# A decoder on one core: the results of sorted expert tiles in a buffer of their own, and the shared experts last in the order

## The chip, the core and the metric

One core of a Trainium2 chip runs the whole program in one launch. The metric is the device time in microseconds. The kernel before was run three times: 835.97, 840.87 and 841.37, median 840.87. The profile is of one more execution, which took 843.06 us and whose span, from its first to its last instruction, is 841.28 us.

## What is computed

Two decoder layers on x of 16 sequences, 128 positions and 256 channels, in fp32. Layer 0: causal attention with one head, attention to a context with 16 heads, and an FFN of 16 blocks of which a router picks four. Layer 1: self attention and windowed attention with 16 heads, and the part that matters here, a mixture of eight experts:

```python
shared_out = _swiglu(x, ws_gate, ws_up, ws_down)           # for every token
scores = jax.nn.sigmoid(x @ gate_weight.T)
topk_w, topk_idx = jax.lax.top_k(scores, 2)                # two of eight experts
topk_w = topk_w / (topk_w.sum(-1, keepdims=True) + 1e-20) * 2.5
g = jnp.einsum('th,eih->tei', x, w_gate)
u = jnp.einsum('th,eih->tei', x, w_up)
y = jnp.einsum('tei,ehi->teh', jax.nn.silu(g) * u, w_down)
out = jnp.einsum('te,teh->th', combine, y) + shared_out    # combine holds topk_w
```

and `x = x + out`.

## The kernel before

The 16 sequences are cut into eight *lanes* of two sequences. A lane is a chain of stages, each a Python generator; up to five lanes are under way at once. The order of instructions on every engine is fixed when the program is built: `Turns` keeps, for each engine, the time up to which it has been given work, and, for each kind of buffer, when its slots come free (`LIMITS`, line 383: six of `p`, four of `xe`, four PSUM banks `bank`, three of `tmp`). Each `yield ENGINE, dict(tag=n)` asks for an engine and for n slots; `q.give(tag)` gives one back. `Turns.run` takes the request that can start first, and at equal times the one of lower *rank*; that is the number that `q.start(generator, rank, at)` sets. Its estimates of cost only set the order: on the chip each engine goes through its own list in that order and waits on semaphores.

The last FFN is done in two ways.

*Dense* (`expert_ffn`, lanes 5, 6 and 7; tensors x5 to x7): all eight experts and the two shared ones, ten rounds of `gu` (four matmuls of 128x256, two for the gate and two for the up projection), `sg` (tanh on ACT), two DVE operations to `hm`, and for the eight experts `wb`, a matmul that spreads the token's weight, with one more DVE operation. Ten matmuls `y` per sequence and a sum on DVE end it, then a store of the lane to the output.

*Sorted* (lanes 0 to 4): `routing` sends each token's row to its two experts' places in DRAM (`to_experts`, indirect DMAs on POOL). When all five lanes are routed, `plan` works out 27 tiles of 128 rows with one expert each, and `sorted_experts` runs `expert_tile` 27 times: two gathers by indirect DMA on POOL (768 columns of the expert's weights, 256 of the rows), transposes `xgt`, a copy `xgT` on ACT, matmuls `gu2`, `sg2` on ACT, two DVE operations to `h2`, a transpose `hT2`, a copy, the matmul `y2`, a copy to the result `yo` on ACT, and a store to `by_experts` in DRAM, issued by ACT. Weights, rows and result share one buffer of kind `p`, 1024 columns wide: the result overwrites the rows, behind the weights. Kind `p` also holds the exponentials of the attentions. `xe` holds `xgT`.

`shared` does the two shared experts of a sorted lane (`gu`, `y1` with `L_shared`); it is started by `layer_1` when the lane is routed. When all five shared parts and all 27 tiles are done (`part_ended`), `combining` starts for the five lanes: a few small DVE operations for the places, four gathers from `by_experts` per lane on POOL (20 in all), a DVE sum for each, and a store of the lane to the output on SP.

In the profile a tile goes by its name without number: `we<-in_L_experts` and `we<-to_experts` are the two gathers, `by_experts<-we` the store, `yg` combining's gathers, `gu<-we,xgT` the matmuls gu2, `y<-we,hT` y2, `ptt` the transpose of a dense lane's (or layer 0's) router weights, `kb` the spread keys of an attention. Most instructions have the line of a helper (135 matmul, 140 transpose, 144 DVE, 149 ACT, 155 POOL, 168 indirect DMA, 189 a load or store).

Of the kernel before, what the change touches and what calls it, by code (L numbers as in the profile page):

```python
# [17 lines left out]
B, S, D = 16, 128, 256  # L18
P = 128
DC = D // P  # L20
G = 2
NL = B // G
# [52 lines left out]
PE, DVE, ACT, POOL, SP = "PE", "DVE", "ACT", "POOL", "SP"  # L75
# [197 lines left out]
def decoder(ctx: ExitStack, tc: tile.TileContext, a: dict, out: bass.AP):  # L273
# [10 lines left out]
    def bank(shape, name):  # L284
        return ps.tile(shape, F32, tag="bank", name=name)
# [101 lines left out]
    q = Turns(nc, LIMITS)  # L387

    def new(tag, shape, name, dtype=F32):
        return work.tile(shape, dtype, tag=tag, name=name, bufs=LIMITS[tag])  # L390

    def normalise(src, free=False):

        yield DVE
        mv = small.tile([P, G, 2], F32, tag="mv", name="mv")
        for j in range(G):
            st = small.tile([P, 6], F32, tag="st", name="st")
            q.dve("bn_stats", st, src[:, j, :])
            q.dve("bn_aggr", mv[:, j, :], st)
        yield POOL  # L400
        rstd = small.tile([P, G], F32, tag="rstd", name="rstd")
        q.pool("tensor_scalar", rstd, mv[:, :, 1], EPS, None, ALU.add)
        q.pool("tensor_tensor", rstd, rstd, power, ALU.pow)

        less = small.tile([P, G], F32, tag="less", name="less")
        q.pool("tensor_tensor", less, mv[:, :, 0], rstd, ALU.mult)
        q.pool("tensor_scalar", less, less, -1.0, None, ALU.mult)
        yield DVE, dict(xn=1)
        xn = new("xn", [P, G, D], "xn")

        def one(j):
            if j:
                yield ACT
                q.act("activation", xn[:, j, :], src[:, j, :], AF.Identity, bias=less[:, j : j + 1], scale=rstd[:, j : j + 1])
            else:
                yield DVE
                q.dve("tensor_scalar", xn[:, j, :], src[:, j, :], mv[:, j, 0:1], rstd[:, j : j + 1], ALU.subtract, ALU.mult)

        yield [one(j) for j in range(G)]
        if free:  # L420
            q.give("xn")
        return xn
# [12 lines left out]
    def transposed(src, free=True):  # L435
        t = yield from transposed_psum(src, free)
        yield ACT, dict(xT=1)
        sb = new("xT", [P, DC, GT], "srcT")
        q.act("copy", sb, t)
        q.give("bank")  # L440
        return sb
# [427 lines left out]
    def self_attention(l):  # L869

        xn = yield from normalise(x[l])
        xT = yield from transposed(xn, free=False)

        def residual():
            for j in range(G):

                yield POOL
                q.pool("tensor_tensor", xn[:, j, :], xn[:, j, :], row("L1_attn_b_o"), ALU.add)
                q.pool("tensor_tensor", x[l][:, j, :], x[l][:, j, :], xn[:, j, :], ALU.add)
            q.give("xn")  # L880

        def of_keys():
            kT = yield from keys(w["qkv"], D, xT, "L1_attn_b_k")
            return (yield from spread(kT))

        kb, qT, v, _ = yield [
            of_keys(),
            queries(w["qkv"], 0, xT, "L1_attn_b_q", 0.0625),
            values(w["qkv"], 2 * D, xT, "L1_attn_b_v"),
            residual(),  # L890
        ]
        q.give("xT")

        def one(j):
            on = yield from attention(qT, kb, v, j)
            yield from output_projection(on, w["o1"], l, j, free="on")

        yield [one(j) for j in range(G)]
        q.give("qk")
        q.give("kb")  # L900
        q.give("v")
        v_tiles.append(v)
# [108 lines left out]
    def shared(l):  # L1011

        g = group_of[l]

        xT = yield from transposed((yield from normalise(x[l])))
        yield PE, dict(hm=1)
        hm = new("hm", [P, DC, GT], "hm1")

        def one(f):
            yield PE, dict(bank=1, tmp=1)  # L1020
            gu = bank([P, 2, GT], "gu")
            for n in range(2):
                at = n * D + f * P
                for d in range(DC):
                    q.matmul(gu[:, n, :], w["shared"][:, d, at : at + P], xT[:, d, :], start=d == 0, stop=d == DC - 1)
            yield from gated(gu, hm[:, f, :])

        yield [one(f) for f in range(DC)]
        q.give("xT")
        for j in range(G):  # L1030
            yield PE, dict(bank=1)
            y = bank([P, D], "y1")
            for f in range(DC):
                q.matmul(y, hm[:, f, j * S : (j + 1) * S], w["shared"][:, f, 2 * D :], start=f == 0, stop=f == DC - 1)
            if j == G - 1:
                q.give("hm")
            yield DVE
            q.dve("tensor_tensor", x[l][:, j, :], x[l][:, j, :], y, ALU.add)
            q.give("bank")
        part_ended(g)  # L1040

    def part_ended(g):

        g.parts -= 1
        if g.parts == 0:
            at = q.now.at
            for l in g.lanes:
                q.start(combining(g, l), 2 * NL + l, at)
# [44 lines left out]
    def expert_tile(g, i):  # L1093

        yield POOL, dict(p=1)

        we = new("p", [P, HC, S], "we").rearrange("p h s -> p (h s)")
        xg = yo = we[:, 3 * D :]
        q.indexed(we[:, 0 : 3 * D], None, a["L1_experts"], g.tile_weights[:, i : i + 1])
        yield POOL  # L1100
        q.indexed(xg, None, g.to_experts, g.tile_rows[:, i : i + 1])
        yield PE, dict(bank=1)
        t = bank([P, DC, S], "xgt")
        for d in range(DC):
            q.transpose(t[:, d, :], xg[:, d * P : (d + 1) * P], ident)
        yield ACT, dict(xe=1)
        xgT = new("xe", [P, DC, S], "xgT")
        q.act("copy", xgT, t)
        q.give("bank")
        yield PE, dict(bank=1, tmp=1)  # L1110
        gu = bank([P, 2, P], "gu2")
        for d in range(DC):
            wt = we[:, d * D : (d + 1) * D].rearrange("p (n f) -> p n f", f=P)
            q.matmul(gu, xgT[:, d, :], wt, start=d == 0, stop=d == DC - 1)
        q.give("xe")
        yield ACT
        sg = new("tmp", [P, P], "sg2")
        q.act("activation", sg, gu[:, 0, :], AF.Tanh, scale=0.5)
        yield DVE, dict(p0=1)
        h = new("p0", [P, P], "h2")  # L1120
        q.dve("scalar_tensor_tensor", sg, sg, 1.0, gu[:, 0, :], ALU.add, ALU.mult)
        q.dve("scalar_tensor_tensor", h, sg, 0.5, gu[:, 1, :], ALU.mult, ALU.mult)
        q.give("tmp")
        q.give("bank")
        yield PE, dict(bank=1)
        t = bank([P, P], "hT2")
        q.transpose(t, h, ident)
        q.give("p0")
        yield ACT, dict(pT0=1)
        hT = new("pT0", [P, P], "hT")  # L1130
        q.act("copy", hT, t)
        q.give("bank")
        yield PE, dict(bank=1)
        y = bank([P, D], "y2")
        q.matmul(y, hT, we[:, DC * D : 3 * D], start=True, stop=True)
        q.give("pT0")
        yield ACT
        q.act("copy", yo, y)
        q.give("bank")
        q.load(g.by_experts[i * P : (i + 1) * P, :], yo, engine=ACT)  # L1140
        q.give("p")

    def combining(g, l):

# [40 lines left out]
    def gated(gu, h):  # L1185

        yield ACT
        sg = new("tmp", [P, GT], "sg")
        q.act("activation", sg, gu[:, 0, :], AF.Tanh, scale=0.5)
        yield DVE  # L1190
        q.dve("scalar_tensor_tensor", sg, sg, 1.0, gu[:, 0, :], ALU.add, ALU.mult)
        q.dve("scalar_tensor_tensor", h, sg, 0.5, gu[:, 1, :], ALU.mult, ALU.mult)
        q.give("tmp")
        q.give("bank")
# [122 lines left out]
    def sorted_experts(g):  # L1317
        yield from plan(g)
        yield [expert_tile(g, i) for i in range(g.tiles)]
        part_ended(g)  # L1320
# [86 lines left out]
    def layer_1(l):  # L1407
        yield from self_attention(l)
        yield from windowed_attention(l)
        ended.append((1, l))  # L1410
        g = group_of.get(l)
        if g is not None:
            yield from routing(l)
            g.left -= 1
            at = q.now.at
            q.start(shared(l), 2 * NL + l, at)
            if g.left == 0:
                q.start(sorted_experts(g), 2 * NL + min(g.lanes), at)

# [127 lines left out]
```

## Time and profile before

| What | us |
|---|---|
| runs, median of three | 840.87 (835.97 to 841.37) |
| profiled execution | 843.06, span 841.28 |
| TensorE (PE) busy | 782.0 (93%) |
| DVE, ACT, POOL busy | 479.2, 393.0, 450.4 |
| first and last gather of an expert tile issued | 649.0, 778.5 |
| last store of a tile issued | 800.55 |
| combining's first and last gather issued | 804.76, 828.67 |
| last matmul, last output store issued | 833.5, 837.9 |

The times in the traces are counted from the span's start. In the page, "busy" is an engine's time in instructions; "PE" is matmuls and "PEld" the loads of their weights, which run beside them. A matmul in fp32 has two records. In the timeline a line is: start, duration, engine, line, operation, out<-in, count, and in brackets how long the engine had been idle before it and what ended that. In the list of waits a line is: who waited, for what, total us, how often, longest. The granted clock of PE was 0.979 in the mean.

### The profile page before, as it was taken

To read this page: it belongs to the slowest core of one execution; us is meant where nothing else is said; L and a number is where in the kernel's file an instruction comes from. 1 tells how busy PE (TensorE), PEld (TensorE's weight loads), DVE (VectorE), ACT (ScalarE), POOL (GpSimd) and SP (SyncE) were. 2 spreads that over 40 slices of the span, in tenths; PEclk is the share of its full clock that TensorE was granted. 3 is DMA by queue.
4 is the path that set the end of the run, shared out by engine and by line. 5 is a ranking of instruction groups with operands and counts; after the bars stand their busy time and mean duration, and the time that the engine had idled before them with its cause. 6 is when DMAs were issued, how large, how long until landed. Compare 5 with 4: busy or idle time off the path is not lost.

```text
span 841.3 us, 19812 instructions
## 1 busy us (share of the span) xinstructions
PE 782.0 (93%) x7886; PEld 617.5 (73%) x7886; DVE 479.2 (57%) x1257; ACT 393.0 (47%) x874; POOL 450.4 (54%) x720
## 2 busy tenths in 40 slices
PE   6999999999999999999999999999878699989984
PEld 5777678878778677777777777777656477877862
DVE  4455636546626537656785478578485553364263
ACT  4545355344355364646652755646545234333310
POOL 5325535514335266566776756966764843474053
PEclk9999899999999999999999999999999999999997
DMA  8457440601201011010013111101201533455133
GB/s 287 157 149 221 133 134 29 182 17 35 57 3 38 14 58 33 15 51 14 20 46 128 63 44 52 59 26 51 77 21 32 163 101 111 129 163 164 57 93 119
DMA packets 60940, 70.41 MB, mean 84 GB/s; under 512 B 8848, under 2 KB 52496, under 8 KB 60208
## 3 DMA queue, kind: packets, MB, share of 16 engines
q1 hardware_dynamic: 51584, 46.20, 17.7%
q0 software_dynamic: 5376, 19.40, 7.9%
q10 hardware_dynamic: 3888, 3.54, 1.2%
q8 instruction: 62, 1.02, 0.5%
q14 instruction: 30, 0.25, 0.1%
HBM read 43.96 MB, written 20.97 MB: 77 GB/s over the span
## 4 chain that ended last, share of the span: by engine, by line
PE 76%; DVE 9%; POOL 5%; ACT 4%; issue 3%; another core or an unknown queue 2%; DMA 0%; ACTq 0%; POOLq 0%; DVEq 0%
PE s L135 15%; PE y L135 11%; PE pj L135 11%; PE gu L135 8%; PE pr L135 8%; PE hp L135 8%; PE oT L135 5%; PE tps L140 3%; PE o L140 2%; ACT p L149 2%; DVE top L144 1%; PE rt L135 1%; DVE x L144 1%; POOL rstd L155 1%
## 5 line engine op out<-in xcount | busy, mean ns | idle before, releaser
L144 DVE TENSOR_REDUCE top<-s 128x8 f32<-128x1024 f32 x96 | 113.0, 1218 | 54.4 <-PE s L135 49.9
L149 ACT ACTIVATE p<-s 128x1024 f32<-128x1024 f32 x96 | 95.2, 1024 | 63.7 <-PE s L135 58.4
L155 POOL TENSOR_TENSOR qs<-qT,less 128x512 f32<-128x512 f32 x48 | 61.6, 1288 | 67.9 <-ACT less L149 60.9
L155 POOL TENSOR_SCALAR rstd<-mv 128x2 f32<-128x2 f32 x77 | 18.5, 241 | 95.1 <-DVE mv L144 88.8
L135 PE MATMUL s<-qs,kb 32*128 32x128 f32 x1536 | 62.1, 290 | 7.6 <-POOL qs L155 3.8
L135 PEld LDWEIGHTS s<-qs,kb 32*128 32x128 f32 x1536 | 51.8, 191 | 22.2 <-issue 7.0
L135 PE MATMUL hp<-srcT,L_w 128*128 128x256 f32 x256 | 67.6, 394 | 0.0
L135 PE MATMUL s<-kb,qT 32*128 32x256 f32 x768 | 61.7, 407 | 3.2 <-DVE top L144 3.0
L135 PE MATMUL y<-L_w,hm 128*128 128x256 f32 x256 | 58.8, 383 | 0.7 <-ACT gained L149 0.6
L155 POOL TENSOR_TENSOR rstd<-rstd,power 128x2 f32<-128x2 f32 x77 | 55.1, 716 | 6.4
L149 ACT ACTIVATE sg<-gu 128x256 f32<-128x256 f32 (+1 forms) x67 | 22.7, 341 | 73.8 <-PE gu L135 57.0
L155 POOL TENSOR_SCALAR kb<-kT,consts 128x256 f32<-128x256 f32 x96 | 53.4, 567 | 6.9 <-ACT kT L149 6.0
L149 ACT ACTIVATE hm<-hp,cols 128x256 f32<-128x256 f32 x64 | 26.8, 470 | 60.9 <-PE hp L135 60.8
L135 PE MATMUL oT<-p,v 128*32 128x128 f32 x1536 | 53.6, 281 | 1.3 <-ACT gained L149 0.9
L135 PEld LDWEIGHTS hp<-srcT,L_w 128*128 128x128 f32 x256 | 45.3, 195 | 12.2 <-issue 2.8
L168 POOL DMA_INDIRECT we<-in_L_experts,tile_weights x27 | 26.2, 971 | 52.2 <-DMA by_experts<-we 13.2
L135 PEld LDWEIGHTS y<-L_w,hm 128*128 128x128 f32 x256 | 47.7, 190 | 8.4 <-issue 1.1
L135 PEld LDWEIGHTS s<-kb,qT 32*128 32x128 f32 x768 | 38.3, 186 | 19.9 <-issue 8.6
L144 DVE SCALAR_TENSOR_TENSOR sg<-sg,gu 128x256 f32<-128x256 f32 (+1 forms) x67 | 24.3, 363 | 45.6 <-ACT sg L149 42.6
L135 PEld LDWEIGHTS oT<-p,v 128*32 128x32 f32 x1536 | 40.1, 112 | 12.6 <-issue 8.1
L135 PE MATMUL gu<-srcT,gu 128*128 128x256 f32 x192 | 47.5, 394 | 1.3 <-DVE hm L144 0.6
L144 DVE TENSOR_TENSOR x<-x,y 128x256 f32<-128x256 f32 x32 | 13.3, 417 | 61.3 <-PE y L135 50.5
(211 smaller groups left out, 1822.0 us busy)
## 6 DMA issues: line engine op xcount, KB each, us to landing
to_experts<-zero SPq DMA_DIRECT2D x7, 1280.0 KB
unseen<-hidden SPq DMA_DIRECT2D x128, 64.0 KB
c<-in_ctx SPq DMA_DIRECT2D x16, 256.0 KB
by_experts<-we ACTq DMA_DIRECT2D x27, 128.0 KB
x<-in_x SPq DMA_DIRECT2D x8, 256.0 KB
L_w<-in_L_w SPq DMA_DIRECT2D x2, 1024.0 KB
hidden<-plain SPq DMA_DIRECT2D x32, 64.0 KB
swap<-kT SPq DMA_DIRECT2D x16, 128.0 KB
```

The costliest lines, as they stand in the source:

```text
L135: self.nc.tensor.matmul(out, lhsT, rhs, **kw)
L140: self.nc.tensor.transpose(out, src, ident)
L144: getattr(self.nc.vector, name)(out, *args, **kw)
L149: getattr(self.nc.scalar, name)(out, *args, **kw)
L155: getattr(self.nc.gpsimd, name)(out, *args, **kw)
L168: self.nc.gpsimd.indirect_dma_start(out, at(out_index), src, at(src_index))
```

## The change

```diff
 def expert_tile(g, i):
         yield POOL, dict(p=1)
 
         we = new("p", [P, HC, S], "we").rearrange("p h s -> p (h s)")
-        xg = yo = we[:, 3 * D :]
+        xg = we[:, 3 * D :]
         q.indexed(we[:, 0 : 3 * D], None, a["L1_experts"], g.tile_weights[:, i : i + 1])
...
         y = bank([P, D], "y2")
         q.matmul(y, hT, we[:, DC * D : 3 * D], start=True, stop=True)
         q.give("pT0")
-        yield ACT
+        q.give("p")
+        yield ACT, dict(xe=1)
+        yo = new("xe", [P, D], "yo")
         q.act("copy", yo, y)
         q.give("bank")
         q.load(g.by_experts[i * P : (i + 1) * P, :], yo, engine=ACT)
-        q.give("p")
+        q.give("xe")
...
 def layer_1(l):
             g.left -= 1
             at = q.now.at
-            q.start(shared(l), 2 * NL + l, at)
+            q.start(shared(l), 2 * NL + l + NL, at)
             if g.left == 0:
                 q.start(sorted_experts(g), 2 * NL + min(g.lanes), at)
```

The result `yo` gets a slot of kind `xe`, of which there are four and which `xgT` uses too; the slot of kind `p` is given back when `y2` has been given to PE. The rank of `shared(l)` goes from 16+l to 24+l, behind the sorted tiles (16), combining (16 to 20) and the dense lanes (21 to 23). Nothing else is edited; since the order of all engines follows from these requests, it changes on every engine from about 630 us on.

## The prediction

> **What bounds the kernel now.** I read the page first: the engines' shares and the chain that ended last.
>
> ```profile
> PE 782.0 (93%) x7886; PEld 617.5 (73%) x7886; DVE 479.2 (57%) x1257; ACT 393.0 (47%) x874; POOL 450.4 (54%) x720
> PE 76%; DVE 9%; POOL 5%; ACT 4%; issue 3%; another core or an unknown queue 2%; DMA 0%; ACTq 0%; POOLq 0%; DVEq 0%
> ```
>
> TensorE is 93% busy and holds 76% of the chain, so its work, which the change leaves alone, is the floor. Only its idle time can be won. The view of stretches, 5 us each, says where that lies (columns: length, then PE, PEld, DVE, ACT, POOL busy, clock, DMA share, GB/s).
>
> ```profile
> 665.00:670.00 5.00, 0.00 (x0) 0.00 (x0) 2.78 (x8) 0.28 (x1) 4.81 (x8) 0.89 0.60 177
> 670.00:675.00 5.00, 3.42 (x11) 2.64 (x12) 2.14 (x9) 1.01 (x3) 4.08 (x6) 0.50 0.23 62
> ...
> 800.00:805.00 5.00, 5.00 (x26) 4.27 (x25) 3.81 (x16) 1.23 (x4) 0.24 (x1) 1.00 0.09 30
> 805.00:810.00 5.00, 4.70 (x22) 3.44 (x21) 4.60 (x19) 1.15 (x3) 3.78 (x5) 1.00 0.27 79
> 810.00:815.00 5.00, 4.52 (x22) 3.81 (x22) 4.39 (x12) 0.38 (x1) 3.78 (x5) 1.00 0.44 123
> 815.00:820.00 5.00, 2.47 (x12) 1.83 (x10) 0.00 (x0) 0.38 (x1) 3.78 (x5) 1.00 0.46 140
> 820.00:825.00 5.00, 4.11 (x12) 3.12 (x13) 3.73 (x9) 0.00 (x0) 3.78 (x5) 0.75 0.50 150
> 825.00:830.00 5.00, 2.80 (x10) 2.07 (x10) 0.00 (x0) 0.00 (x0) 3.70 (x4) 0.91 0.38 113
> 830.00:835.00 5.00, 2.45 (x5) 0.87 (x4) 1.87 (x5) 0.00 (x0) 0.00 (x0) 0.77 0.13 37
> 835.00:840.00 5.00, 0.00 (x0) 0.00 (x0) 2.80 (x7) 0.00 (x0) 0.00 (x0) 0.50 0.57 200
> ```
>
> From 640 to 700 PE idles 11.4 us, from 700 to 800 only 3.9, and from 800 to its end at 834.2 another 8.2; then 7.1 us pass without it. The timeline shows what that tail is, and the waits what the change touches.
>
> ```profile
> 800.55 0.33 ACTq L189 DMA_DIRECT2D by_experts<-we  x1
> 804.76 0.95 POOL L168 DMA_INDIRECT yg<-by_experts,results  x1 [25.30 <-DVE results L144]
> 818.94 0.38 ACT L149 ACTIVATE sg<-gu 128x256 f32<-128x256 f32 x1 [5.28 <-remote]
> 820.36 0.42 DVE L144 TENSOR_TENSOR hm<-wb,hm 128x256 f32<-128x256 f32 x1 [5.40 <-remote]
> 828.67 0.95 POOL L168 DMA_INDIRECT yg<-by_experts,results  x1 [0.30 <-issue]
> 833.10 0.42 DVE L144 TENSOR_TENSOR x<-x,y 128x256 f32<-128x256 f32 x1 [8.90 <-remote]
> 837.94 0.37 SPq L1169 DMA_DIRECT2D out_x<-x  x1
> ```
>
> ```profile
> POOL we L168 <- DMA by_experts<-we: 13.5, 7, 3.7
> PE ptt L135 <- DVE chosen L144: 6.6, 1, 6.6
> ```
>
> The last expert tile is stored at 800.55. Only then can combining run: 20 gathers at 1.25 us on POOL, 804.76 to 829.6, the sums on DVE, the last output at 837.94. PE has too little left to fill that time. And three waits, each on a PE result that the records show as long done, last 5.3, 5.4 and 8.9 us. The profile does not name what ends them ("remote").
>
> **The change, part by part.**
>
> *The result's own buffer.* A tile's result goes to a slot of xe, and its weight buffer (one of six of p) is free after matmul y2, not after the copy (0.37 us) and the landing of the store. No instruction is added. POOL's waits on the store, 13.5 us in 7, go; late next is y2 itself, which POOL then waits for. POOL is 54% busy and not the bound, so this is worth nothing by itself: it only lets tiles start sooner. New is that xe, four slots, now serves twice per tile, so that ACT may wait in line for a store at the copy to xgT or yo, with the gates queued behind and PE behind those. In the written order at least eight ACT instructions lie between a store and the wait for it, some 3.5 us or more at ACT's 0.45 us each (393.0/874); the store's waits above are 1.9 us in the mean, 3.7 at most. Bounds 0 to 3.7; I take 0, by the mean.
>
> *Shared experts last.* The order of instructions moves from about 630 us on. I compared the two written orders behind the last y2. Before: 28 matmuls gu, 7 wb, 20 y. After: 44 gu, 9 wb, 40 y. From the chain, the 10 matmuls y of one sequence take 4.32 us and 4 gu 1.73, so 0.43 each; a wb is half that. Before, 12.1+1.5+8.6 = 22.2 us of PE work lie behind the last tile; after, 19.0+1.9+17.3 = 38.2, which is a whole dense lane and the end of another. The last tile comes 16 us of PE work earlier. Combining needs 4.2 us to its first gather, 25 for 20 gathers, some 2 to land, 0.5 for the last sum and 3.4 for the store: 35 us. It now lies beside 38 us of PE. DVE has in that stretch 10 rounds of 3x0.42, 20 sums of 0.48, 20 small operations of 0.2 and four sums of 0.42, or 28 of 38 us: room, if what it waits for is on time.
>
> The sum, against the profiled execution (843.1 us; span 841.3):
> 1. PE's idle time behind 800 falls from 8.2 us. The undisturbed stretch 800 to 810 idles 0.3 in 10; 21 us of gu and wb at that rate are 0.6, and as DVE's sums stand between rounds I take 2.0. Gain 6.2; bounds 0 (the late results stay) and 7.6.
> 2. From PE's end to the span's end: now 7.1 us, since sums stand behind PE's last result. After, it is one sum (0.42), its hops and the 3.4 us from DVE's last end (837.9) to the span's: 3.9. Gain 3.2; bounds 0 and 3.2.
> 3. The clock. The three stretches at 0.75 to 0.91 behind 820 cost, busy time by the missing share, 1.0+0.3+0.6 = 1.9 us; each follows or holds idle PE. I take a gain of 0.8, as some idle time stays; bounds 0 and 1.9.
> 4. The middle. PE's largest wait, 6.6 us at ptt, is a dense lane's router. Ahead of it two shared gu groups (3.5), six shared y (2.6), and the first tiles' xgt and gu (2.3) leave: PE is there 8.4 us sooner. What it waits for also comes sooner: the multiplication eq stands behind 6 gathers instead of 9, and no longer behind two rotary operations: 3x1.25+1.28+1.27 = 6.3 us. So the wait grows by 2.1 us. The keys' spreading (kb) moves back, past three more gathers and a 1.7 us norm: 668.3 to 673.7, done by 676, where PE asked for it at 679.8: covered, with 4 us to spare; without that cover PE pays up to 5.4. SP's queue keeps its order but for an output: 0. Bounds of all this: a gain of 6.6 (the wait goes) and a loss of 6.6 (another one like it). I take a loss of 2.1.
>
> Sum: 6.2+3.2+0.8-2.1 = 8.1, so 843.1-8.1 = 835.0 for such an execution. The median of the runs, 840.87, lies 2.2 us under it; I carry that over: **832.8**.
>
> Term 3 by the page: the row is that PE stands still in 665:670 and has a clock of 0.50 in the next stretch. The Trainium skill ("TensorE: Matmul & The Clock Gate", "What's actually happening") says that an idle window of about 3.4 us halves the clock and a busy one restores it. The trace agrees. By it term 3 would be the full 1.9, and 831.7 the time, if nothing idles in the tail; but it speaks against the change in the middle, where a longer wait at ptt stays at half clock afterwards.
>
> **The rivals.**
> - *The late results come again, as they were.* For it: they fall in 813 to 833, within the run of gathers or PE's last 45 matmuls, and both conditions remain. Against: the first seven gathers run without them. If the same three waits meet the end, terms 1 to 3 shrink to about 2 and cover term 4: near 840.9 (839 to 842).
> - *Slower: the late results catch the loop.* Beside the gathers there now stands a loop of ten rounds PE, ACT, DVE, PE over four banks, in place of 40 matmuls that wait for little. If every fourth round, when the banks are full, waits 5.3 to 8.9 us as the three did, three such waits cost 16 to 27 us: 849 to 860. It turns slower than before by over 1% once they exceed 8.1+8.4 = 16.5 us together. Against it: no such wait stands anywhere else in 841 us.
> - *Combining was not the bound in the timed runs.* The runs spread from 835.97 to 841.37; the low one is about 5 us under the others, as if without the 8.9 us wait. Then the gain is some 4 us: 836.7.
> - *More is won in the middle:* the 6.6 us wait goes with its half clock, and instead of losing 2.1 the change wins 2 to 6.6: 824 to 829.
>
> **How the numbers follow.** Forecast (828 to 837): 0.40. Late results as before: 0.23. Late results in the loop: 0.15. Combining not the bound: 0.10. Won in the middle: 0.12. One per cent, about what a measurement can tell from no change, is 8.4 us: below 832.5 is faster. Of the forecast's 0.40 I give 0.18 to faster, as its centre lies just above, and 0.22 to within 1%. Faster: 0.18+0.12 = 0.30; same: 0.22+0.23+0.10 = 0.55; slower: 0.15. The range 825 to 847 leaves out the lowest part of the last case and most of the loop's.
>
> **What would show it.** Right: the last by_experts store near 786 us, the last gather before PE's last gu, an output store of a dense lane as the very last, PE idle under 3 us in its last 38, PE's end within 4 us of the span's. POOL's wait on by_experts gone, ACT with no wait on it over 1 us. Term 4: the wait at ptt between 6 and 9 us, no wait of PE on kb. Wrong, if "remote" waits stand beside the gathers again, if the last store still lies at 800 or later, or if the middle has a second wait of PE over 3 us.

## The result, and the profile after

| | us, median (range) | to the kernel before |
|---|---|---|
| kernel before, beside the changed one | 838.74 (835.28 to 841.56, 10 runs) | |
| changed kernel | 831.09 (827.16 to 834.86, 10 runs) | 0.9895, 95% interval 0.9865 to 0.9926 |

The profiled execution of the changed kernel took 827.16 us, its span is 825.4 (before: 843.06 and 841.28). Three of the ten runs of the kernel before are those quoted at the start, and the chip of these first runs and profiles is not on record. The two profiled executions lie far apart: 843.06 is above all ten runs of the kernel before, 827.16 is the fastest of the ten of the changed kernel, so the profiles differ by 15.9 us and the medians by 7.7. On another chip, below, the same kernel was 0.5% slower than the kernel before, and that is the larger part of what there is to learn here.

First the page of the changed kernel, engines and the chain that ended last:

```profile
PE 777.8 (94%) x7886; PEld 617.3 (75%) x7886; DVE 478.4 (58%) x1257; ACT 393.0 (48%) x874; POOL 450.4 (55%) x720
PE 77%; DVE 7%; POOL 6%; ACT 4%; issue 3%; DMA 1%; ACTq 0%; DVEq 0%; POOLq 0%
```

The work is the same; the entry "another core or an unknown queue" has gone from the chain. Then its view of stretches (columns as in the prediction; the first two rows hold the longest wait at ptt):

```profile
650.00:655.00 5.00, 2.15 (x10) 1.54 (x9) 4.66 (x13) 0.00 (x0) 4.60 (x6) 0.95 0.68 233
655.00:660.00 5.00, 3.02 (x9) 2.48 (x10) 2.19 (x10) 0.37 (x1) 3.78 (x5) 0.50 0.66 188
...
790.00:795.00 5.00, 5.00 (x26) 4.31 (x25) 2.95 (x7) 0.77 (x2) 3.78 (x5) 1.00 0.62 186
795.00:800.00 5.00, 3.01 (x15) 2.18 (x13) 1.84 (x6) 0.77 (x2) 3.82 (x4) 1.00 0.45 132
800.00:805.00 5.00, 5.00 (x16) 3.91 (x17) 4.90 (x14) 0.38 (x1) 3.90 (x4) 0.66 0.55 166
805.00:810.00 5.00, 5.00 (x27) 4.16 (x26) 4.11 (x11) 1.15 (x3) 3.78 (x4) 1.00 0.64 191
810.00:815.00 5.00, 5.00 (x26) 4.25 (x25) 4.65 (x13) 0.77 (x2) 0.00 (x0) 1.00 0.28 90
820.00:825.00 5.00, 1.56 (x8) 1.02 (x6) 0.42 (x1) 0.00 (x0) 0.00 (x0) 1.00 0.15 52
```

PE works through the gathers, with 2.0 us of idle time in one stretch (795 to 800) and a lower clock in the next; in the last stretch it is busy until its end at 821.6. The timeline of the same tail:

```profile
780.63 0.33 ACTq L189 DMA_DIRECT2D by_experts<-yo  x1
784.82 0.94 POOL L168 DMA_INDIRECT yg<-by_experts,results  x1 [23.91 <-DVE results L144]
798.29 0.48 DVE L144 SCALAR_TENSOR_TENSOR x<-yg,weight,x 128x256 f32<-128x256 f32 x1 [3.12 <-DMA yg<-by_experts,results]
808.90 0.95 POOL L168 DMA_INDIRECT yg<-by_experts,results  x1 [0.30 <-issue]
810.92 1.89 PE L135 MATMUL gu<-srcT,L_shared 128*128 128x256 f32 x8
821.59 0.42 DVE L144 TENSOR_TENSOR x<-x,y 128x256 f32<-128x256 f32 x1 [3.89 <-PE y L135]
822.04 0.37 SPq L1317 DMA_DIRECT2D out_x<-x  x1
```

The last store lies at 780.63 instead of 800.55, the last gather stands ahead of PE's last gu, and the last output is that of a dense lane (line 1317). No engine waits for "remote". The waits of POOL and PE:

```profile
POOL we L168 <- PE hT L140: 18.8, 6, 6.1
POOL we L168 <- PE y L135: 9.3, 5, 2.8
```

```profile
PE ptt L135 <- DVE chosen L144: 6.3, 2, 4.8
```

POOL no longer waits for a store but for PE: for y2, as the prediction said, and longer for hT, which it did not name. The tail came out close to the forecast.

### The profile page after: what moved, and what is told of

The parts are those of the page before. It is cut to its first block, busy times and chain, and to the rows that moved or that the text cites. A ratio compares the mean times of both kernels' runs of the same rounds, so it can differ in the third digit from the quotient of the medians.

```text
span 825.4 us, 19793 instructions
## 1 busy us (share of the span) xinstructions
PE 777.8 (94%) x7886; PEld 617.3 (75%) x7886; DVE 478.4 (58%) x1257; ACT 393.0 (48%) x874; POOL 450.4 (55%) x720
## 4 chain that ended last, share of the span: by engine, by line
PE 77%; DVE 7%; POOL 6%; ACT 4%; issue 3%; DMA 1%; ACTq 0%; DVEq 0%; POOLq 0%
PE s L135 15%; PE pj L135 11%; PE y L135 11%; PE gu L135 10%; PE pr L135 9%; PE hp L135 8%; PE oT L135 4%; PE tps L140 3%; PE o L140 2%; ACT p L149 2%; DVE top L144 2%; POOL rstd L155 2%; PE rt L135 1%; POOL we L168 1%; POOL qs L155 1%
## 5 line engine op out<-in xcount | busy, mean ns | idle before, releaser
L135 PE MATMUL oT<-p,v 128*32 128x128 f32 x1536 | 52.6, 278 | 0.8 <-ACT gained L149 0.5
L140 PE MATMUL tps<-consts,xn 128*128 128x128 f32 x244 | 38.4, 282 | 10.3 <-DVE xn L144 7.2
```

Of the source, the lines that this page charges most:

```text
L135: self.nc.tensor.matmul(out, lhsT, rhs, **kw)
L140: self.nc.tensor.transpose(out, src, ident)
```

## The experiments

All times of a trace count from the span's start. Up to its 6000th matmul, at some 567 us, all these kernels have one written order. "PE idle" is counted behind the last by_experts store, "behind PE" is from PE's end to the span's end. "Late" is how long after the modelled end of a group gu behind the last store ACT started the sg that reads it, at most: 0.04 us is the normal hop. "Late before" is the longest delay of a PE signal between 640 and 760 us, worked out from the trace's semaphore events: the update's time less the nearest end before it of a matmul that gives a signal.

| Run | chip | ratio to before, 95% | span, us | last store | PE idle | behind PE | late | late before |
|---|---|---|---|---|---|---|---|---|
| before, first profile | - | | 841.3 | 800.5 | 8.1 | 7.1 | 4.6 | 1.3 |
| changed, first profile | - | 0.9895 (0.9865 to 0.9926) | 825.4 | 780.6 | 2.0 | 3.8 | 0.04 | 0.12 |
| before_again | 9 | one run, 845.44 us | 843.7 | 805.8 | 0.8 | 15.3 | 0.04 | 0.12 |
| after_again | 9 | one run, 829.96 us | 828.2 | 783.6 | 2.7 | 3.8 | 0.04 | 0.12 |
| buffer_only | 9 | 0.9815 (0.9777 to 0.9853) | 830.0 | 793.7 | 0.0 | 5.5 | 0.04 | 0.12 |
| order_only | 9 | 0.9908 (0.9875 to 0.9942) | 835.0 | 798.0 | 0.8 | 11.4 | 0.04 | 0.25 |
| after_b | 5 | 1.0054 (1.0030 to 1.0078) | 849.3 | 789.9 | 12.9 | 3.8 | 17.4 | 2.1 |
| buffer_only_b | 5 | 0.9997 (0.9978 to 1.0016) | 842.0 | 788.9 | 15.5 | 3.8 | 16.8 | 1.4 |
| half_before | 5 | 0.9945 (0.9924 to 0.9966) | 836.5 | 799.0 | 7.4 | 3.8 | 0.04 | 1.5 |
| half_after | 5 | 0.9942 (0.9920 to 0.9965) | 838.8 | 789.4 | 5.3 | 3.8 | 5.0 | 2.0 |
| direct_after | 4 | 0.9834 (0.9797 to 0.9871) | 825.9 | 785.5 | 0.0 | 3.6 | 0.04 | 1.4 |
| paced_after | 4 | 1.0031 (1.0013 to 1.0049) | 843.1 | 786.7 | 8.7 | 3.8 | 0.04 | 2.1 |
| paced3_after | 0 | 0.9968 (0.9953 to 0.9982) | 839.1 | 787.7 | 6.4 | 3.8 | 0.04 | 2.0 |
| paced_lane | 0 | 0.9953 (0.9935 to 0.9971) | 838.3 | 788.3 | 6.8 | 3.8 | 0.04 | 2.1 |

The kernel before had medians of 841.56 (chip 9), 844.09 (5), 843.44 (4) and 843.19 (0). A ratio rests on 4 (direct_after) to 12 runs of the kernel named.

### Both kernels once more

*before_again* is the kernel before, *after_again* the changed kernel, unedited.

> The kernel before, once more, unchanged, for a second profile. Theory A (the three waits of 5.3, 5.4 and 8.9 us whose end the profile does not name are a property of this tail): they come again beside the gathers, and the span is 838 to 843 us. Theory B (they befall some executions only): no such wait over 2 us, and with the last sum no longer held up the span ends some 5 us earlier, 833 to 837 us, although the order is the same.

> The changed kernel once more, for a second profile. Theory A of the unnamed waits: they belong to the tail of the kernel before, so none here, span 824 to 828 us. Theory B (any execution can have them): if they come, they catch the loop of the last dense lane beside the gathers and the span is over 835 us. The first 590 us have the same order in both kernels; the two profiles so far differ there by 3.2 us, and this one shows whether that is chance (it then lies anywhere within 4 us).

The unnamed waits did not come back in before_again: theory B, they do not belong to the order of the kernel before. Yet it took no less time: its span is 843.7 us, where theory B had 833 to 837. In after_again no such wait stands either, and its span is 828.2. Up to the 6000th matmul, where all have one order, the profiles of both kernels and of their parts range over 5 us (565.7 to 570.6), so the 3.2 us between the first two are chance. The stretches of before_again show why it was not faster:

```profile
820.00:825.00 5.00, 5.00 (x25) 4.41 (x24) 3.16 (x8) 0.00 (x1) 3.93 (x4) 1.00 0.64 192
825.00:830.00 5.00, 3.33 (x16) 2.59 (x14) 1.84 (x6) 0.00 (x0) 3.78 (x5) 1.00 0.52 157
830.00:835.00 5.00, 0.00 (x0) 0.00 (x0) 2.59 (x6) 0.00 (x0) 3.78 (x5) 0.66 0.56 161
835.00:840.00 5.00, 0.00 (x0) 0.00 (x0) 1.12 (x3) 0.00 (x0) 0.12 (x1) 0.50 0.46 146
```

PE ran with 0.8 us of idle time and ended at 828.3; the gathers on POOL and the sums on DVE went on by themselves to 838.4. Here combining sets the end. In the first profile, too, its sums end last, but the last of them stand behind a sum that waited 8.9 us for a late result of PE.

### Each part alone

*buffer_only* is the changed kernel with the old rank, *order_only* the kernel before with the new one:

```diff
 buffer_only, against the changed kernel
-            q.start(shared(l), 2 * NL + l + NL, at)
+            q.start(shared(l), 2 * NL + l, at)
 order_only, against the kernel before
-            q.start(shared(l), 2 * NL + l, at)
+            q.start(shared(l), 2 * NL + l + NL, at)
```

> The result's own buffer without the new rank. Theory 1 (what counts is the PE work behind the last tile, which has to cover 35 us of combining): the written order leaves 40 gu, 8 wb and 30 y there, 31.8 us against 22.2 before and 38.2 after, so of the 13 us that lacked 3 still lack: three quarters of the gain, about 833 us, a tail in which PE idles some 3 us. Theory 2 (the gain is in the middle, from where the shared parts stand): nearly no gain, 837 to 839. Theory 3 (the gain is POOL's 13.5 us of waits on the store): all of it, 831.

> The new rank without the result's own buffer. Theory 1: 36 gu, 8 wb and 20 y behind the last tile are 25.8 us, 9 us short of combining's 35: a quarter to a third of the gain, about 836 us, PE idle some 6 to 8 us behind the last tile. Theory 2: most of the gain, 831 to 833. Theory 3: none, 838 to 839, and POOL's waits on the store stay at 10 us or more.

The order alone fits theory 1 by its time (835.23 us, 836 expected), though what is uncovered lies behind PE's end and not in its idle time. The buffer alone, 826.91, beat all three; theory 1 had it at 833. Counted from the 6000th matmul the profiles have 272.4 and 275.1 us for the kernel before, 266.8 for the order, 259.4 for the buffer, 259.7 and 262.0 for both. So the buffer, which the prediction called worth nothing by itself, does on this chip what the whole change does. Theory 1's mechanism holds: a slot of p that is free earlier in the written order draws the tiles forward and leaves 31.8 us of PE's work behind the last one instead of 22.2, and what PE does not cover behind the last store shrinks from 15.2 and 16.1 us to 5.5; with the order alone it is 12.1, with both 5.8 and 6.5. It is not all of the gain: of the 15.7 us between before_again and buffer_only, 10.6 are this, and 5.2 are busy time of PE (236.0 and 230.8 us), of which 29.0 and 19.8 us passed at a clock of 0.50. Whether the new rank costs anything on top, on such a chip, one run of after_again does not settle.

### The same two on another chip

*after_b* is the changed kernel, *buffer_only_b* is buffer_only, both on chip 5.

> The changed kernel once more, beside buffer_only_b on the same chip. The traces so far, counted from the last PE instruction that has the same place in all written orders (some 567 us), take 259.7 and 262.0 us for the changed kernel and 259.4 for the buffer alone, and 5.8, 6.6 and 5.5 us of these lie uncovered by PE behind the last tile's store. Theory 1 (the tail): once the PE work left behind the last tile (32 us for the buffer alone, 38 for both) is near the 36 us that combining takes, more of it gives nothing; the two kernels are equal within 2 us, both near 0.985 of the kernel before. Theory 2 (the new place of the shared experts costs on top of the buffer, in the middle): this kernel is 3 to 5 us slower than the buffer alone, as 0.9895 against 0.9815 in runs on two chips would have it.

> The buffer of its own with the shared experts at their old place. Theory 1: equal to the full change within 2 us, near 0.985 of before (828 where before is 840). Theory 2: 3 to 5 us faster than the full change, near 0.981.

Neither theory's ratio: the changed kernel is slower than the one before, 849.92 us against 844.09 (12 and 30 runs), the buffer alone equals it at 843.85. The changed kernel is 6.1 us slower than the buffer alone, a little more than theory 2's 3 to 5. The stretches of after_b and its timeline:

```profile
800.00:805.00 5.00, 5.00 (x25) 4.16 (x23) 1.33 (x3) 0.18 (x1) 3.78 (x5) 1.00 0.67 207
805.00:810.00 5.00, 2.19 (x9) 1.54 (x9) 1.63 (x4) 0.20 (x1) 3.78 (x5) 1.00 0.36 102
810.00:815.00 5.00, 0.00 (x0) 0.00 (x0) 0.00 (x0) 0.00 (x0) 3.78 (x5) 0.82 0.36 104
815.00:820.00 5.00, 2.94 (x7) 2.12 (x7) 1.97 (x5) 0.39 (x1) 3.07 (x4) 0.50 0.47 145
820.00:825.00 5.00, 1.96 (x5) 0.93 (x5) 2.01 (x6) 0.94 (x3) 0.00 (x0) 0.50 0.08 24
825.00:830.00 5.00, 5.00 (x13) 3.83 (x13) 4.29 (x12) 0.38 (x1) 0.00 (x0) 0.50 0.16 54
```

```profile
799.74 3.62 PE L135 MATMUL gu<-srcT,gu 128*128 128x256 f32 x16
803.30 1.89 PE L135 MATMUL gu<-srcT,gu 128*128 128x256 f32 x8
804.82 0.38 ACT L149 ACTIVATE sg<-gu 128x256 f32<-128x256 f32 x1 [13.13 <-PE wb L135]
815.47 0.39 ACT L149 ACTIVATE sg<-gu 128x256 f32<-128x256 f32 x1 [10.27 <-remote]
816.17 0.42 DVE L144 TENSOR_TENSOR hm<-wb,hm 128x256 f32<-128x256 f32 x1 [9.26 <-remote]
816.64 0.37 PE L135 MATMUL wb<-selT,experts 128*128 128x256 bf16 x1 [8.48 <-issue]
822.54 0.94 ACT L149 ACTIVATE sg<-gu 128x256 f32<-128x256 f32 x3 [6.68 <-PE gu L135]
```

From 810 to 815 nobody works but POOL, which issues gathers. To read why, pair each group gu with its sg. The first two groups end on PE at 801.63 and 803.36 (16 records, eight to a group); ACT starts their sg at 804.82 and 815.47. The next two end at 805.19 and 808.16; their sg come at 822.54 and 822.82, when the gathers are over: 17.4 and 14.7 us late. PE then stands still: its four banks hold three groups gu and a wb (803.36 to 808.16) whose readers have not been told. Four signals arrive within 0.22 us (822.52 to 822.74), among them those of three groups gu, whose matmuls take at least 1.8 us each: the work had been done, and the signals came late. The end of a matmul in the trace is a modelled one; the Trainium skill says so too ("Perfetto Trace Analysis", "Summary: the profiler window per engine type"): the end is estimated and the passing on of the signal is hidden. So the trace shows the delay only at the readers. POOL's gathers run from 794.1 to 819.0 us; the last late signal comes 3.8 us after the last of them has ended on POOL.

Compared with the first profile of the changed kernel, from the 6000th matmul on after_b takes 279.5 us instead of 259.7. Of these 19.8 us, 10.9 are PE's idle time behind the last store, 4.3 its idle time among the tiles, and 4.6 longer work, mostly because the clock was at 0.50 for 17 us behind the stall. The Trainium skill ("TensorE: Matmul & The Clock Gate", "What's actually happening") has an idle window of some 3.4 us halve the clock; the rows at 0.82 and 0.50 agree, as PE's records stop at 808.2 and the clock halves at 813.2.

Looking back, the first profile of the kernel before came from such an execution as well (late 4.6 us and, for DVE's last sums, 10.2), the first of the changed kernel did not. On a chip with late results the kernel before loses little, 2.5 us from chip 9 to chip 5 (5.4 from the first runs), probably because 20 matmuls y and few rounds of the loop stand beside its gathers; no profile of it on chip 5 shows this. The changed kernel loses 19 there, counted from its first runs, and the buffer alone 17. What parts these two on chip 5 is not idle time (42.7 and 43.5 us from the 6000th matmul on, with what lies behind PE) but longer work, 236.8 us against 231.2: after_b goes on at half clock through rounds of the loop that buffer_only_b, which stood still from 805 to 819, ran later. That is 10.2 us of work at 0.50 behind the last tile against 5.2, or 2.5 us lost; among the tiles it is 19.0 against 15.2, or 1.9 us, and after_b idles 1.8 us more there. So part of the difference does lie in the middle, as theory 2 has it; one profile of each does not settle how much.

### Half the gathers

*half_before* and *half_after* issue only the first of each token's two gathers and add its row twice:

```diff
             yield POOL
-            q.indexed(y[:, i, :], None, g.by_experts, by[:, i : i + 1])
+            if k == 0:
+                q.indexed(y[:, i, :], None, g.by_experts, by[:, i : i + 1])
...
-                "scalar_tensor_tensor", x[l][:, j, :], y[:, i, :], weight[l][:, j, k : k + 1], x[l][:, j, :], ALU.mult, ALU.add
+                "scalar_tensor_tensor", x[l][:, j, :], y[:, j * TOPE, :], weight[l][:, j, k : k + 1], x[l][:, j, :], ALU.mult, ALU.add
```

> The kernel before with 10 of combining's 20 gathers left out: each token's second expert result is not fetched, its sum uses the first one's row again, so all 20 sums on DVE and all of PE's work stay. PE's written order keeps 22 us of work behind the last tile. Theory A (combining sets the end): ten gathers of 1.25 us come off the chain, 12.5 us, so that 36 to 41 us behind the last store become 24 to 28 and PE's 22 us cover nearly all of it: 10 us less than before, about 830. Theory B (PE and its late results set the end; in one of the two profiles of before PE idles only 0.8 us behind the last store): the gathers lie beside PE's work, and what goes is at most the sums behind PE's last result, 0 to 4 us: 836 to 840.

> The changed kernel with the same 10 gathers left out (each token's second expert result is not fetched, and the first one's row is added again). Theory A: PE's 38 us behind the last tile already cover combining, so only the 5.8 to 6.6 us not covered by PE can move, and of these the 3.8 behind PE's end stay, as a dense lane's sum and store end it: 0 to 2 us less than the changed kernel, about 829 to 831. Theory B (the gathers' traffic or combining's sums still hold up the loop beside them): 4 us less or more, 827 or lower.

half_after took 840.24 us, 9.7 less than after_b: theory B by the difference (4 us or more), though not by the time, as 827 or less stood for a chip without late results. The latest result is 5.0 us late instead of 17.4. half_before took 840.00, 4.1 less than before: theory B's 0 to 4 just fits, theory A's 10 does not. Its gathers end at 815.5, PE only at 832.7, after 7.4 us of idle time in which it waited for DVE's hm, which stood behind sums that themselves waited for their gathers:

```profile
PE gu L135 <- DVE hm L144: 5.6, 3, 3.5
DVE x L144 <- DMA yg<-by_experts,results: 4.1, 5, 1.9
```

The two runs are not a pure count of gathers: without them the order is planned anew, and behind the last store it differs from that of the kernel with all gathers at 36 places on DVE and 4 on PE in half_before, at 40 and 10 in half_after. In half_before no result is late behind the last store, though its gathers follow each other at the same 1.25 us, and a gu that ended 8.9 us behind the first of them was read at once. What spares that one run of ten is open.

### Who holds the signals up

*direct_after* replaces the indirect gathers by plain loads of the same size from SP. PE, DVE and ACT keep the changed kernel's written order:

```diff
             yield POOL
-            q.indexed(y[:, i, :], None, g.by_experts, by[:, i : i + 1])
+            q.charge(POOL, 1050.0)
+            q.moved(4 * P * D)
+            q.now.at += 2000.0
+            c = 26 - (l * G * TOPE + i) % 27
+            nc.sync.dma_start(y[:, i, :], g.by_experts[c * P : (c + 1) * P, :])
```

> The changed kernel with combining's 20 indirect gathers on POOL replaced by 20 plain loads of the same size (128 KB, whole tiles from by_experts, the last tile first) issued by SP; it leaves the choice of rows out, so the sums add other rows. The written order of PE, ACT and DVE is that of the changed kernel. In after_b, PE's results behind the last store reached ACT and DVE up to 17 us after the modelled end of the matmul, from 7 us after the first gather until the gathers ended; in the profile of the changed kernel on another chip none was late. A chip of the first sort shows itself in this trace by results that are 0.5 to 2 us late between 640 and 750 us, beside the tiles' gathers, which stay. Theory P (POOL's indirect DMAs hold up PE's signals): on such a chip no result of PE behind the last store is over 0.5 us late, PE idles less than 4 us there and the time is 0.985 to 0.99 of before. Theory T (the transfers' traffic does): results come 5 to 17 us late as in after_b and the time is 1.00 of before or more. On a chip of the other sort both give 0.985 to 0.99, and nothing is told apart.

The chip shows late results among the tiles (1.4 us, at most of the places where after_b has them). Behind the last store there are none, and its stretches leave PE no gap:

```profile
795.00:800.00 5.00, 5.00 (x25) 4.32 (x24) 3.47 (x9) 0.77 (x2) 0.00 (x0) 1.00 0.56 161
800.00:805.00 5.00, 5.00 (x26) 4.24 (x25) 4.75 (x14) 1.15 (x3) 0.00 (x0) 1.00 0.66 209
805.00:810.00 5.00, 5.00 (x26) 4.18 (x25) 4.17 (x12) 0.83 (x3) 0.00 (x0) 1.00 0.53 170
```

828.78 us, 0.9834: theory P. The DMAs were as busy as in after_b, where 800 to 805 had 0.67 and 207 GB/s. That speaks against the traffic and for POOL's indirect gathers. Three things stay open. The changed kernel itself was not run on chip 4, which counts as one with late results by its lateness among the tiles alone; half_before, on chip 5, has that too (1.5 us) and no late result in its tail. Whether POOL's part in issuing the gathers or the scattered rows do it, this run does not part, as it changed both. And part of the time has another reason: no sum of DVE waits for a load here, where in the first profile of the changed kernel six waited 6.4 us for gathers.

### Pauses between the gathers

*paced_after* puts five small memsets behind every gather, as the diff shows, *paced3_after* three, *paced_lane* eight behind each lane's fourth (if i == 3) alone:

```diff
             q.indexed(y[:, i, :], None, g.by_experts, by[:, i : i + 1])
+            pause = small.tile([P, 2], F32, tag="pause", name="pause", bufs=1)
+            for _ in range(5):
+                nc.gpsimd.memset(pause, 0.0)
```

> The changed kernel with five memsets of 128x2 on POOL behind each of combining's 20 gathers, some 0.2 us each, so that gathers come about 2.3 us apart instead of 1.25. It costs by itself: the last gather is issued 44 us behind the first, and the span ends 55 to 60 us behind the last store, where the changed kernel took 45 without late results and 59 with them. Theory R (back-to-back issue is what holds PE's signals up): on a chip that shows late results between 640 and 750 us, none behind the last store is over 3 us late, PE ends 41 to 45 us behind the last store, and only combining sets the end: 841 to 850 us. Theory H (any run of gathers holds them up until it ends): results are 10 us late or more, for longer, as the run lasts 45 us; PE ends over 55 us behind the last store, and the time is 853 or more.

> The changed kernel with three memsets of 128x2 on POOL behind each of combining's 20 gathers. By paced_after's rows (five memsets take 0.74 us and the gathers came 1.84 us apart) the gathers are then about 1.55 us apart, and combining takes 4.2 us to the first gather, 31 for the rest of the run, 2 to land, 4 for the last sum and its store: 41 us, which PE's 38 us of work behind the last tile nearly cover. On a chip that shows late results between 640 and 750 us: theory R (back-to-back issue holds PE's signals up, and a short pause lets them pass) expects no result of PE over 1 us late behind the last store and 0.985 to 0.99 of before, near 830 where before is 843; theory R2 (three memsets are too short) expects results 5 to 15 us late, as in after_b, and 1.00 of before. On a chip without late results both expect 0.985 to 0.99.

> The changed kernel with eight memsets of 128x2 on POOL (1.2 us by paced_after's rows) only behind each lane's fourth gather, so that runs of four gathers, 5 us long, take the place of one of 25. In after_b the first late result came 7 us after the first gather. On a chip that shows late results between 640 and 750 us: if lateness builds up over a run of more than 5 us and a pause of 1.2 us clears it, no result is over 2 us late behind the last store and the time is 0.985 to 0.99 of before; if only the share of POOL's time matters, results are 5 to 12 us late and the time is 0.995 to 1.005 of before. On a chip without late results it is 0.985 to 0.99.

All three ran on chips that show late results among the tiles (2.0 to 2.1 us), and in none is a gu late behind the last store: theory R, and for the lanes that a pause of some 1.2 us behind every four gathers, 5 us, is enough. As with direct_after this holds as far as these chips are of the sort of chip 5; the changed kernel without a pause was not run there. It fits the traces where the results were late: the first late gu ended 7.6 us (after_b, half_after) to 8.2 us (buffer_only_b) behind the first gather, and in buffer_only_b those that ended 2.8 to 6.2 us behind it were on time. Whether the length of the pause counts or the memset between two gathers stays open. paced_after's gathers came 1.84 us apart, not 2.3; its time, 845.42, lies in theory R's 841 to 850, but PE ends 52.6 us behind the last store, between R's 41 to 45 and H's 55. The other two took 840.50 and 838.96, where 830 was hoped for. The stretches of paced_lane and its waits between 783 and 845:

```profile
805.00:810.00 5.00, 2.92 (x13) 1.72 (x11) 3.12 (x8) 0.77 (x2) 3.54 (x4) 1.00 0.36 113
810.00:815.00 5.00, 3.97 (x17) 3.07 (x18) 2.48 (x7) 0.38 (x1) 3.36 (x12) 1.00 0.39 115
815.00:820.00 5.00, 3.10 (x14) 2.00 (x12) 4.03 (x10) 0.77 (x2) 3.36 (x12) 1.00 0.31 93
```

```profile
DVE x L144 <- DMA yg<-by_experts,results: 11.3, 10, 2.6
PEld gu L135 <- DVE hm L144: 7.3, 5, 2.7
```

DVE goes through its list in order (the same order in all traces of the changed kernel but half_after). Its sums for combining stand between the operations of the loop, and each that waits for a slower gather keeps the loop's hm, and so PE, waiting behind it. PE idles 6.8 us instead of 12.9. That is not all: against the first profile of the changed kernel, 825.4 us, paced_lane's 838.3 has 4.8 us more idle time behind the last store, 5.5 more among the tiles, which no pause touches (after_b: 4.3), and 3.5 ahead of the 6000th matmul. paced_lane (0.9953) and paced3_after (0.9968) are the only versions that came out under the kernel before on a chip with late results and compute all of it, by less than 0.5%; the buffer alone with the pause was not tried.

## Why the prediction was right, and where it was not

1. *PE's work behind the last tile.* Right. 16 us more of it was to bring the last store from 800.5 to 786; it came to 780.6, of which 3.2 us stem from the part before the 6000th matmul that the change leaves alone.
2. *Terms 1 and 2, PE's idle time and the time behind PE.* Their sum is right, 9.4 forecast, 15.2 to 5.8 us measured, and 16.1 to 6.5 in the pair on chip 9. The split of the 15.2 was one execution's: without late results PE of the kernel before idles 0.8 us, and 15.3 lie behind it.
3. *Term 3, the clock.* 0.8 forecast. One stretch at 0.66 remains, which costs 5.00 x 0.34 = 1.7 us of the 1.9 before: 0.2.
4. *Term 4, the middle.* The wait at ptt was to grow by 2.1; the longest is 4.8 and 6.6 us in the two profiles (with a second one, 6.3 and 8.1 in all), where one of 6.6 and 6.5 stood. PE's idle time from the 6000th matmul to the last store fell, from 24.3 and 23.0 to 21.6 and 22.4. A loss of 2.1 was taken, it was a gain of 0.6 to 2.7: the term had the wrong sign. No PE wait on kb, no ACT wait on by_experts, as forecast.
5. *The buffer, "worth nothing by itself".* Wrong, and the step that failed: that POOL is not the bound says nothing about what a slot of p given back earlier does to the written order. Alone it gains 1.85% on chip 9, the order alone 0.92%.
6. *The rivals.* "Late results come again" and "late results catch the loop" were given 0.38 together, as though each execution drew for itself. On chip 5 the second happened in the profile, and all 12 runs (846.63 to 853.58) lie above the median of the kernel before. The loss there is 5.8 us, where 849 to 860 against 840.87 meant 8 to 19; that 849.92 itself lies in that range is luck, as the kernel before took 844.09 there. It came from 10.9 us of idle time and 4.6 of longer work at a slower clock rather than from three waits of 5 to 9.
7. *The sum.* 8.1 us forecast, 7.7 measured between the medians. Part of that is luck. The profiled pair differs by 15.9: 9.4 of terms 1 and 2, 2.7 of idle time among the tiles, 0.7 of PE's busy time, in which term 3 lies, and 3.2 from the part that the change leaves alone. And that the gain came at all is owed to the chip on which the two kernels were first compared.

So the account: the end is set by whatever is longest behind the last tile's store, combining (36 to 41 us) or PE's remaining work. The change brings that store forward and covers combining with a loop PE, ACT, DVE. The cover is good if the loop runs. On chip 5 the loop's signals came late beside POOL's gathers, and then the cover costs more than it hid. Chips 4 and 0 show late signals among the tiles as chip 5 does, but only versions with pauses or plain loads ran there. That POOL's gathers are what holds the signals up is argued from these runs across chips. What makes a chip one or the other, and whether it stays so, was not tested: each was seen in one session of runs only.

## What to carry to other kernels

Count the engine work that the written order leaves behind the last producer, and ask what kind it is: a loop over three engines covers a run of gathers only if its signals come through. A slot given back earlier is a change of order when a planner hands out slots; compare the written orders of each part of a change before calling it free. And before trusting a few per cent, run both kernels on a second chip.

## What the hardware showed

Beside POOL's indirect gathers, issued back to back every 1.25 us, PE's signals reached ACT and DVE up to 17.4 us after the modelled ends of the matmuls in three of four profiles on chip 5. The first late gu ended 7.6 to 8.2 us behind the first gather, and the last late signals came 2.2 to 3.8 us after the last gather had ended on POOL. In the fourth, half_before, none was late. Among the expert tiles, where up to six gathers follow each other, signals were up to 2.1 us late on chips 5, 4 and 0. With a pause of 0.43 us of memsets behind each gather, or of 1.2 us behind every four, and with plain loads of the same size from SP, none was late behind the last store, on chips 4 and 0. On chip 9, and in the first profile of the changed kernel, gathers at the same pace came with delays of at most 0.25 us.
